# Seven batches' token norms turned block by block in the feed-forward and loaded turned in the slots' stage; the slots' keys and values put in place by masked operations

## The chip, the cores and the metric

The kernel runs as one program on one core of a Trainium2 chip. The core has five engines that run their own instruction queues: TensorE (PE, with its weight loads as PEld), VectorE (DVE), ScalarE (ACT), GpSimd (POOL) and SyncE (SP, which here only issues DMAs). SBUF is the on-chip memory of 128 partitions, PSUM holds the sums of matrix products, and 16 DMA engines move data between SBUF and DRAM. The metric is device time in microseconds (us), the median of several runs. About 0.2% is what a measurement of this kernel can tell from no change.

## The reference

Eight batches of 512 tokens of width 512 pass through a cross-attention with a feed-forward beside it, and then through a slot layer. All is float32.

```python
x = x + tanh(g_xattn) * xattn_and_ff(layernorm(x), ctx, mask, ...)   # attention over ctx, plus silu(gate) * a @ Wff2
yn = layernorm(x)                                                    # the "token norms"
# slot layer on yn: 16 slots, 16 heads of width 32
o = q + mha(slot_query, yn, yn, d_W*)          # each slot attends to all 512 tokens of its batch
h = layernorm(o) * ln_g + ln_b                 # one slot per expert
o = o + (silu(h @ W1[e] + b1) * silu(h @ Wg[e] + bg)) @ W2[e] + b2   # 16 experts of 512 x 2048
out = mha(yn, o, o, c_W*)                      # each token attends to its batch's 16 slots
x = x + tanh(g_ffn) * out
```

## The kernel before

The work is in five stages, each with its own tile pools and an order of instructions that is written out by hand (`manual_schedule`): every engine executes in exactly the order in which the program issues to it, and waits on semaphores where data are not ready.

**Cross-attention** (to about 1050 us): not touched. There is one thing in it that the prediction looks at: `spread` (L348) places 32 x 32 blocks that VectorE has transposed (L338) by small DMAs from SBUF to SBUF.

**Feed-forward** (about 1050 to 2230 us), `for s in range(NB * NFC + 2)`: 16 half batches `j` of 256 tokens, each in 16 steps of some 4.64 us, with a seven-product scheme for matrix products (L840, L864) on TensorE, and sums on VectorE. `settle(j, ...)` returns the jobs that finish half batch `j` during the steps of the next one, keyed by (step, slot): additions of the accumulators, storing of the sum (`keep_sum`), its statistics (`look`, steps 5 and 7), and `norm(t)` (steps 9 and 11, slot 1), which normalises 128 tokens in place (L129) and stores them to DRAM (`yn_kept`, L909). `due(s, slot)` issues a job between two given operations of a step. The last batch has no `norm`; it is normalised later. `settle` also has three scratch tiles `qa`, `qu`, `qw` of 128 x 256 in a pool of one buffer each.

**Slots' stage** (about 2230 to 2320 us). For each batch `b` the scores of the first half of the slots (`slot_scores`, L1179) need the norms with width on the partitions (`places[b]`, four chunks `c`), and the pooling (`slot_pool`, L1218) needs them with tokens on the partitions (`ys[b]`). `load_norm` (L1290) loads the second form from DRAM. `turn_tokens(b, t)` (L1298, L1300, L1302) makes the first out of it by four TensorE transposes for each tile of 128 tokens, and a copy from PSUM to SBUF by ScalarE or VectorE. The turns of batch `b + 1` stand between the score products of batch `b`. The probabilities are transposed by TensorE (`turn_probs`, L1208, L1209) after the third chunk of the next batch's scores. In between, `fetch()` (L1129 and L1125) loads the first pieces of the experts' weights, 2 MB each, into a ring of four buffers; one of the four (`early`) first holds two batches' norms.

**Experts** (about 2320 to 2795 us): 96 pieces of 2 MB stream through the ring (six buffers after a while); each consumed piece issues the next `fetch`. Beside it TensorE does the second half of the slots (`late_slots`, in two-advance steps per piece) and, from advance `SWITCH` to `LAST`, the tokens' queries (`token_queries`, L1487). The last fetches load the matrices of the output attention: `(cwk, cwv)`, `(cwo, bdk)` and `(bdv)`, where `bdk` and `bdv` are block-diagonal forms that start as zeros, written by GpSimd (`memset`, L1136).

**Output attention** (about 2795 us to the end): `slot_side` projects the slots to keys and values (L1672) and writes each head's 32 partitions into its place in `bdk` or `bdv`: three VectorE operations (L1686) and two ScalarE operations (L1681) per half. Then 32 tiles of 128 tokens pass through a pipeline: scores (L1719), their transposes (L1731), a softmax over the 16 slots (`token_scores` L1736 to L1738, `weights` L1744 to L1746), transposes (L1752), the output product (L1761), and `finish` (L1769, L1770).

Of the kernel before, what the change touches and what calls it, by code (L numbers as in the profile page):

```python
# [51 lines left out]
def flamingo_block(  # L52
# [678 lines left out]
    yn_kept = [keep.tile([N, D], F32, name=f"yn_kept_{b}") for b in range(B - 1)]  # L731

    with ExitStack() as sb, tc.manual_schedule(engines=ALL_ENGINES):
        NW = 4
# [143 lines left out]
        def settle(j, xr, acc):  # L878
# [27 lines left out]
            def norm(t):  # L906
                normed(xr[t], xr[t], mv[:, t, 0:1], col(rs, t))
                r = (2 * h + t) * P
                nc.sync.dma_start(yn_kept[b][r : r + P, :], xr[t])  # L909

            def step_q1():
                nc.vector.tensor_scalar(a, part(acc, 1), tg_x, None, ALU.mult)
# [33 lines left out]
            if b < B - 1:  # L946
                jobs[9, 1], jobs[11, 1] = lambda: norm(0), lambda: norm(1)
            return jobs
# [163 lines left out]
    def fetch():  # L1112
        if not pieces:
            return
        kind, e, i = piece = pieces.pop(0)
        pool, tag = buffers.pop(0)
        buffers.append((pool, tag))

        assert kind in ("w1", "wg", "w2") or pool is ring
        name = kind if kind in ("w1", "wg", "w2") else kind[0]  # L1120
        t = pool.tile([P, 8, 512], F32, tag=tag, name=f"{name}_{e}_{i}")
        if kind == "w2":

            w = e_W2[e, i * 1024 : (i + 1) * 1024, :].rearrange("(p k) d -> p (k d)", k=8)
            nc.sync.dma_start(t.rearrange("p q f -> p (q f)"), w)  # L1125
        elif kind in ("w1", "wg"):

            w = (e_W1 if kind == "w1" else e_Wg)[e, i * 256 : (i + 1) * 256, :]
            nc.sync.dma_start(  # L1129
                t.rearrange("p q f -> p (q f)"), w.rearrange("(p k) f -> p (k f)", k=2)  # L1130
            )
        else:
            for k, n in enumerate(kind):
                half = t[:, 4 * k : 4 * k + 4]
                if n in ("bdk", "bdv"):
                    nc.gpsimd.memset(half, 0.0)  # L1136
                else:
                    w = {"cwk": c_Wk, "cwv": c_Wv, "cwo": c_Wo}[n]
                    nc.sync.dma_start(half, rows(w))
                pieces_in[n, 0, 0] = half  # L1140
            return
        pieces_in[piece] = t
# [7 lines left out]
    ball = slots.tile([P, 512], F32, name="ball")  # L1150
    oT = slots.tile([P, ND, P], F32, name="oT")


# [17 lines left out]
    pooled = c1.tile([P, ND, FH, HS, B], F32, name="pooled")  # L1171
    ys, probs, pTs = {}, {}, {}

# [10 lines left out]
    def slot_scores(b, m, sp, apart=False):  # L1184

        yT = places[b].rearrange("p (c n) -> p c n", c=ND)
        for c in range(ND):
# [89 lines left out]
    with ExitStack() as sc, tc.manual_schedule(engines=ALL_ENGINES):  # L1277
        ps = sc.enter_context(tc.tile_pool(name="ps_c", bufs=2, space=PSUM, reuse_waits="tile"))

        def load_norm(b):  # L1280

            at = {4: 7, 5: B}.get(b)
            if b in (2, 3):
                y = early[:, 4 * (b - 2) : 4 * (b - 1)]
            elif at is None:
                y = c3.tile([P, NT, D], F32, tag=f"y{b % 2}", name=f"y_{b}")
            else:
                y = places[at].rearrange("p (t d) -> p t d", t=NT)
            src = yn_kept[b] if b < B - 1 else y_kept[b]
            nc.sync.dma_start(y, src.rearrange("(t p) d -> p t d", p=P))  # L1290
            return y

        def turn_tokens(b, t):
# [3 lines left out]
            for c in range(ND):  # L1297
                nc.tensor.transpose(tp[:, c, :], ys[b][:, t, c * P : (c + 1) * P], ident)  # L1298
            if (t % 2 or b == 0) and (b, t) != (1, NT - 1):
                nc.scalar.copy(yT[:, :, t * P : (t + 1) * P], tp)  # L1300
            else:
                nc.vector.tensor_copy(yT[:, :, t * P : (t + 1) * P], tp)  # L1302
# [8 lines left out]

        early = ring.tile([P, 2 * NT, D], F32, tag=buffers[RING - 1][1], name="early")
        for b in range(4):
            ys[b] = load_norm(b)
        b2r = e1.tile([NS, D], F32, tag="ys", name="b2r")
        nc.sync.dma_start(b2r, e_b2)
        nc.sync.dma_start(o, by_slot(slot_query[0]))
        nc.sync.dma_start(dbo, d_bo.partition_broadcast(P))
        ys[4] = load_norm(4)
        fetch()  # L1320
        ys[5] = load_norm(5)
        for _ in range(RING - 2):
            fetch()
        for i, bvec in enumerate((e_b1, e_bg)):
            nc.sync.dma_start(
                ball[64 * i : 64 * i + 64], bvec.rearrange("e (k f) -> (e k) f", k=4)
            )
# [7 lines left out]
        nc.scalar.activation(col(spark, 0), neg_half[:, 0:1], AF.Exp)  # L1335
        for t in range(NT):
            turn_tokens(0, t)
        for b in range(B):
# [15 lines left out]
            for t in range(NT):  # L1354
                if t == NT - 1 and b > 0:
                    turn_probs(b - 1, 0, bank4("tp", f"stp_{b - 1}"))
                next(late)
                if b + 1 < B and (b != 1 or t > 0):
                    turn_tokens(b + 1, t)
                if b == 0 and t == NT - 1:  # L1360
                    turn_tokens(2, 0)
            if b > 0:
                for _ in slot_pool(b - 1, [bank4("pl", f"pl_{b - 1}")]):
                    pass
            if b in (1, 2):
                ys[b + 5] = load_norm(b + 5)
            if b == 4:
                fetch()
# [3 lines left out]
            if b == B - 1:  # L1372
                dwo = c3.tile([P, 4, D], F32, tag="y0", name="dwo")
                nc.sync.dma_start(dwo, rows(d_Wo))
        late = slot_scores(1, 1, bank("sc", "lsc_1"), apart=True)
        for c in range(ND):
# [13 lines left out]
    with experts_scope, ExitStack() as se, tc.manual_schedule(engines=ALL_ENGINES):  # L1390
# [41 lines left out]
        def prepare():  # L1432
            for j in range(2):
                nc.vector.memset(held[j], 0.0)
            nc.vector.tensor_add(fold, ident[:, 0:32], ident[:, 32:64])
            nc.vector.tensor_add(fold, fold, ident[:, 64:96])
# [56 lines left out]

        SWITCH, LAG, LAST = 82, 6, PIECES - 1
        AHEAD = 3
# [155 lines left out]

    bdk, bdv = (t.rearrange("p g (b r s) -> p g b r s", b=B, r=4) for t in (bdk, bdv))


    with ring_scope, ExitStack() as sd, tc.manual_schedule(engines=ALL_ENGINES):
# [9 lines left out]
        def slot_side(w, bd, bias, name, half):  # L1665

            kp = ps.tile([P, 2, NS, B], F32, tag="mm", name=f"{name}_p_{half}")
            gs = slice(2 * half, 2 * half + 2)
            for i in range(2):
                g = 2 * half + i  # L1670
                for c in range(ND):
                    nc.tensor.matmul(  # L1672
                        kp[:, i].rearrange("p s b -> p (s b)"), lhsT=w[:, c, g * P : (g + 1) * P],
                        rhs=oT[:, c, :], start=(c == 0), stop=(c == ND - 1),
                    )
            for r in range(4):
                s = slice(FD * r, FD * r + FD)
                if r == 3:
                    for i in range(2):
                        g = 2 * half + i  # L1680
                        nc.scalar.activation(  # L1681
                            bd[s, g, :, r, :].rearrange("p b s -> p s b"), kp[s, i],
                            AF.Identity, bias=bias[s, g : g + 1],
                        )
                else:
                    nc.vector.tensor_tensor(  # L1686
                        bd[s, gs, :, r, :].rearrange("p g b s -> p g s b"), kp[s],
                        wide(bias[s, gs], NS, B), ALU.add,
                    )

        def slot_values(b, m):
# [4 lines left out]
            for i in range(2):  # L1696
                g = 2 * m + i
                nc.tensor.matmul(
                    vp[64 * i : 64 * i + 64, :],
                    lhsT=bdv[:, g, b].rearrange("p r s -> p (r s)"), rhs=cwo[:, g, :],  # L1700
                    start=True, stop=True,
# [3 lines left out]
        def load(i):  # L1705
            b, t = divmod(i, NT)
            xr = d7.tile([P, D], F32, tag="xr", name=f"xr_d_{i}")
            nc.sync.dma_start(xr, y_kept[b][t * P : (t + 1) * P, :])
            return xr

        def batch_scores(b, m):
# [5 lines left out]
            for i in range(2):  # L1717
                g = 2 * m + i
                nc.tensor.matmul(  # L1719
                    sp[64 * i : 64 * i + 64, :],  # L1720
                    lhsT=bdk[:, g, b].rearrange("p r s -> p (r s)"), rhs=qT[:, g, :],
                    start=True, stop=True,
# [3 lines left out]
        def token_scores(i):  # L1726
            b, t = divmod(i, NT)
            sp = ps.tile([P, FH, NS], F32, tag="sc", name=f"sc_{i}")
            spf = sp.rearrange("p h s -> p (h s)")
            for m in range(2):  # L1730
                nc.tensor.transpose(  # L1731
                    spf[:, m * P : (m + 1) * P], sTs[b][:, m, t * P : (t + 1) * P], ident
                )
            mx = d4.tile([P, FH], F32, tag="mx", name="mx")
            pr = d4.tile([P, FH, NS], F32, tag="pr", name=f"pr_{i}")
            nc.vector.tensor_reduce(mx, sp, AX.X, ALU.max)  # L1736
            nc.vector.tensor_tensor(pr, sp, wide(mx, NS), ALU.subtract)
            nc.scalar.activation(pr, pr, AF.Exp, scale=FSCALE)  # L1738
            return pr

        def weights(pr):
            den = d4.tile([P, FH], F32, tag="den", name="den_d")
            rden = d4.tile([P, FH], F32, tag="rden", name="rden_d")
            nc.vector.tensor_reduce(den, pr, AX.X, ALU.add)  # L1744
            nc.vector.reciprocal(rden, den)
            nc.gpsimd.tensor_tensor(pr, pr, wide(rden, NS), ALU.mult)  # L1746

        def turn_weights(i, pr):
            prf = pr.rearrange("p h s -> p (h s)")
            tp = ps.tile([P, 2, P], F32, tag="tp", name=f"ptp_{i}")  # L1750
# [103 lines left out]
```

## Time and profile before

| | |
|---|---|
| Time, median of 3 runs | 2927.24 us (2927.17 to 2928.19) |
| Profiled execution, its own time | 2923.94 us |
| Its span, first to last instruction | 2922.1 us |
| Granted TensorE clock, mean | 0.998 |
| Busy: PE, DVE, ACT, POOL | 2843.3, 1781.0, 833.1, 1043.3 us |
| Moved by DMA | 481.26 MB, mean 165 GB/s |

A profile's part with 40 slices shows the share of each engine's busy time by stage; TensorE is busy throughout, while the DMA engines are busy in the cross-attention, nearly idle in the feed-forward, and full from about 2330 to 2795 us. A line of the "timeline" gives start, duration, engine, line of the code, operation, output <- inputs, shapes, a count of merged instructions, and in brackets how long the engine had been idle and who released it. SPq lines are issues of DMAs, not their transfers. The merged durations of TensorE overlap, so steps are best read from start to start. A float32 product shows as two records.

### The profile page before, as it was taken

How to read it: one execution, taken by the hardware profiler on the slowest of the kernel's cores; microseconds unless marked ns; L12 is line 12 of the kernel's file. 1: busy time of each engine (PE TensorE's matmuls, PEld its weight loads, DVE VectorE, ACT ScalarE, POOL GpSimd, SP SyncE). 2: the span in 40 equal slices, each digit the busy share in tenths (PEclk: the TensorE clock that was granted, in tenths of full speed). 3: DMA queues.
4: the chain of work that ended last, by engine and by line, in shares of the span. 5: the costliest groups of instructions: out<-in, count | busy, mean ns of one | idle time of the engine just before them, and what ended most of it. 6: DMA issues, size and time to landing. Idle time of an engine off the chain costs nothing.

```text
span 2922.1 us, 49771 instructions
## 1 busy us (share of the span) xinstructions
PE 2843.3 (97%) x17822; PEld 1824.2 (62%) x17822; DVE 1781.0 (61%) x5337; ACT 833.1 (29%) x2256; POOL 1043.3 (36%) x835
## 2 busy tenths in 40 slices
PE   9999999999999999999999999999999998899898
PEld 5333333333333489999999999999998644322233
DVE  7887878878786766666666666666665312111145
ACT  4444444444444521111111111111112222000023
POOL 6888888788887671000000000000001100000034
PEclk9999999999999999999999999999999999999999
DMA  7887877778788650000000000000005399999954
GB/s 207 202 205 177 213 184 194 197 187 213 180 204 197 160 213 24 26 30 30 30 30 30 30 30 27 29 30 30 30 23 213 125 426 426 425 427 426 427 182 150
DMA packets 262584, 481.26 MB, mean 165 GB/s; under 512 B 24832, under 2 KB 195360, under 8 KB 249024
## 3 DMA queue, kind: packets, MB, share of 16 engines
q1 hardware_dynamic: 261616, 476.10, 51.5%
q8 instruction: 141, 2.31, 0.3%
q0 software_dynamic: 480, 1.57, 0.1%
q14 instruction: 107, 0.88, 0.1%
q10 hardware_dynamic: 240, 0.40, 0.1%
HBM read 303.91 MB, written 40.89 MB: 118 GB/s over the span
## 4 chain that ended last, share of the span: by engine, by line
PE 85%; DMA 11%; DVE 2%; issue 1%; SPq 1%; ACT 0%; POOL 0%; POOLq 0%; DVEq 0%; ACTq 0%
PE p L840 27%; PE acc L864 13%; DMA w<-in_L_ffn_e_W_dram 9%; PE sim L296 8%; PE qp L279 8%; PE av L374 7%; PE op L388 7%; PE out L1761 2%; PE p_w L1565 1%; PE pl L1218 1%; DMA cwk<-in_L_ffn_c_Wv_dram 1%; PE ssc L1179 1%; PE lsc L1179 1%; PE kp L250 1%; PE tp L216 1%; PE p_wg L1565 1%
## 5 line engine op out<-in xcount | busy, mean ns | idle before, releaser
L323 POOL TENSOR_SCALAR pr<-pr,rden 128x512 f32<-128x512 f32 x504 | 788.3, 1582 | 175.5 <-DVE rden L316 173.9
L310 ACT ACTIVATE pr<-pr,nmx 128x512 f32<-128x512 f32 x512 | 363.5, 711 | 375.7 <-DVE nmx L307 330.7
L307 DVE CUSTOM_DVE_ANT_0 pr<-sim,bias 128x512 f32<-128x512 f32 x512 | 322.8, 685 | 74.2 <-PE sim L296 74.2
L338 DVE STREAM_TRANSPOSE turned<-pr 128x512 f32<-128x512 f32 x504 | 322.3, 682 | 9.2 <-DMA pT<-turned 1.2
L840 PE MATMUL p<-xs,w1g 128*128 128x128 f32 x2048 | 312.3, 275 | 0.5 <-DMA w1g<-in_L_xattn_Wff_dram 0.5
L840 PE MATMUL p<-ts,s 128*128 128x128 f32 x2048 | 311.5, 275 | 0.0
L864 PE MATMUL acc<-w,ht 128*128 128x256 f32 x1024 | 305.5, 381 | 0.0
L840 PEld LDWEIGHTS p<-ts,s 128*128 128x128 f32 x2048 | 289.1, 192 | 13.0
L840 PEld LDWEIGHTS p<-xs,w1g 128*128 128x128 f32 x2048 | 279.6, 192 | 7.1 <-issue 0.6
L296 PE MATMUL sim<-kT,q 64*128 64x512 f32 x1024 | 263.8, 616 | 2.8 <-DVE nmx L307 2.5
L892 POOL TENSOR_TENSOR xr_b<-xr_b,qa 128x256 f32<-128x256 f32 x16 | 11.7, 731 | 678.7 <-DVE xr_b L889 678.7
L279 PE MATMUL qp<-xnT,wq 128*128 128x512 f32 x496 | 245.1, 618 | 0.6 <-DVE xnT L238 0.6
L374 PE MATMUL av<-pT,v 128*64 128x512 f32 x1008 | 233.3, 605 | 0.3 <-issue 0.3
L388 PE MATMUL op<-wo,o 128*128 128x512 f32 x512 | 230.6, 593 | 0.0
L864 PE MATMUL acc<-t,ht 128*128 128x256 f32 x768 | 229.1, 380 | 0.0
L296 PEld LDWEIGHTS sim<-kT,q 64*128 64x128 f32 x1024 | 91.3, 186 | 168.6 <-issue 102.2
L1072 DVE TENSOR_TENSOR c<-p,w 128x128 f32<-128x128 f32 x256 | 74.4, 291 | 179.5 <-PE p L840 179.1
L1066 ACT ACTIVATE g<-p 128x128 f32<-128x128 f32 x256 | 70.9, 277 | 388.3 <-PE p L840 388.3
L1078 ACT ACTIVATE g<-g 128x128 f32<-128x128 f32 x256 | 79.4, 310 | 354.9 <-DVE g L1077 354.9
L279 PEld LDWEIGHTS qp<-xnT,wq 128*128 128x128 f32 x496 | 84.3, 189 | 151.7 <-issue 142.6
L388 PEld LDWEIGHTS op<-wo,o 128*128 128x128 f32 x512 | 95.2, 190 | 112.6 <-issue 112.3
L840 PEld LDWEIGHTS p<-ts,w1a 128*128 128x128 f32 x1024 | 154.4, 191 | 13.3
(306 smaller groups left out, 4174.8 us busy)
## 6 DMA issues: line engine op xcount, KB each, us to landing
w<-in_L_ffn_e_W_dram SPq DMA_DIRECT2D x64, 2048.0 KB, 17.5
pT<-turned SPq DMA_DIRECT2D x1008, 128.0 KB, 2.8
wg<-in_L_ffn_e_Wg_dram SPq DMA_DIRECT2D x32, 2048.0 KB, 28.0
wq<-in_L_xattn_Wq_dram SPq DMA_DIRECT2D x64, 256.0 KB, 4.6
xn<-in_x_dram SPq DMA_DIRECT2D x32, 256.0 KB, 3.0
cn<-in_ctx_dram SPq DMA_DIRECT2D x32, 256.0 KB, 3.8
xnT_kept<-xnT SPq DMA_DIRECT2D x8, 1024.0 KB
xr<-in_x_dram SPq DMA_DIRECT2D x32, 256.0 KB, 4.8
```

The source lines that it names most:

```text
L279: nc.tensor.matmul(qp, lhsT=w[:, c, :], rhs=xnT[:, c, :], start=(c == 0), stop=(c == ND - 1))
L296: nc.tensor.matmul(sps[l, e], lhsT=qs[half * HP + l][r, t * P : (t + 1) * P], rhs=kT[r, :], start=True, stop=True,)
L307: nc.vector.tensor_tensor_reduce(pr, sps[l, e], bias, -XSCALE, LARGE, ALU.add, ALU.min, nmx)
L310: nc.scalar.activation(pr, pr, AF.Exp, bias=nmx, scale=-1.0, accum_out=dens[l][:, e : e + 1])
L323: nc.gpsimd.tensor_scalar(prs[l, e], prs[l, e], rden[:, e : e + 1], None, ALU.mult)
L338: nc.vector.transpose(turned[:, :, hd, :], pr.rearrange("p (j c) -> p j c", c=32))
L374: nc.tensor.matmul(av[XD * e : XD * e + XD], lhsT=v[:, j, :], rhs=p5[:, j, :, :, e, :], start=(j == 0), stop=(j == NT - 1),)
L388: nc.tensor.matmul(op, lhsT=o[:, l, :], rhs=wo[:, half * HP + l, :], start=(l == 0), stop=(l == HP - 1),)
L840: nc.tensor.matmul(psum[:, 0:HN], lhsT=w[:, c, :], rhs=x[:, c, :], start=(first and c == 0), stop=(last and c == 1), skip_group_check=True,)
L864: nc.tensor.matmul(part(acc, q), lhsT=ht[:, idx, :], rhs=rhs, start=(kp == 0 and half == 0), stop=(kp == NFC // 2 - 1), skip_group_check=True,
L1072: nc.vector.tensor_tensor(c22, p7[:, 0:HN], w, ALU.add)
L1078: nc.scalar.activation(g2, g2, AF.Silu)
```

## The change

1. In the feed-forward, `norm` moves one step earlier (8 and 10). A new job `turn` (steps 9 and 11) has VectorE transpose the 32 x 32 blocks of the tile's two halves into `z` tiles, which reuse the buffers of `qa` and `qu`, and stores each by four DMAs to DRAM (`yT_kept`, width by tokens). This is done for batches 0 to 6: 28 tiles, 56 transposes, 224 stores.
2. In the slots' stage, batches 0 to 6 are loaded turned (`load_turned`); only batch 7 is still turned by TensorE (16 transposes instead of 128). The loads of all tokens' norms are issued ahead of the first fetches. Batches 0 and 1 are first loaded into other buffers (`home`) and loaded once more to their places later. Two ring buffers hold the early norms instead of one; two fetches follow them, and the third and fourth come after the pooling at `b == 2` and `b == 4`.
3. `bdk` and `bdv` are no longer zeroed. `own_head`, 1 where a partition belongs to head `r` of its group and 0 elsewhere, masks the result: two VectorE operations of 128 x 512 per half write (sum + bias) x mask over whole tiles. The order within them is batch, slot, head instead of batch, head, slot, so the right side of the projections is read with a stride, and the softmax in `token_scores` and `weights` runs over a stride of four.
4. `LAST` becomes `PIECES - 3`, so the tokens' queries are spread over two advances less.

```diff
+    yT_kept = [keep.tile([D, N], F32, name=f"yT_kept_{b}") for b in range(B - 1)]
...
+            def turn(t):
+                r = (2 * h + t) * P
+                yT = yT_kept[b].rearrange("(k i) n -> i k n", i=32)
+                for i, n in enumerate("au"):
+                    z = b0.tile([P, HD], F32, tag=f"q{n}", name=f"z{n}_{j}_{t}")
+                    nc.vector.transpose(z, xr[t][:, i * HD : (i + 1) * HD])
+                    for k in range(4):
+                        nc.sync.dma_start(
+                            yT[:, 8 * i : 8 * i + 8, r + 32 * k : r + 32 * k + 32],
+                            z[32 * k : 32 * k + 32].rearrange("p (k c) -> p k c", c=32),
+                        )
...
-                jobs[9, 1], jobs[11, 1] = lambda: norm(0), lambda: norm(1)
+                jobs[8, 1], jobs[10, 1] = lambda: norm(0), lambda: norm(1)
+                jobs[9, 1], jobs[11, 1] = lambda: turn(0), lambda: turn(1)
...
-                if n in ("bdk", "bdv"):
-                    nc.gpsimd.memset(half, 0.0)
-                else:
+                if n not in ("bdk", "bdv"):
...
-        yT = places[b].rearrange("p (c n) -> p c n", c=ND)
+        yT = turned.get(b, places[b]).rearrange("p (c n) -> p c n", c=ND)
...
+        for b in (0, 1):
+            turned[b] = home(b, b)
+            load_turned(b, turned[b])
+        early = [
+            ring.tile([P, 2, NT * D], F32, tag=buffers[RING - 2 + i][1], name=f"early_{i}")
+            for i in range(2)
+        ]
         for b in range(4):
-            ys[b] = load_norm(b)
+            load_norm(b, early[b // 2][:, b % 2])
...
-        ys[4] = load_norm(4)
-        fetch()
-        ys[5] = load_norm(5)
+        load_turned(2, places[2])
+        load_turned(3, places[3])
+        load_norm(4, places[7])
+        load_turned(4, places[4])
+        load_norm(5, places[B])
+        load_norm(6, home(0, 6))
+        load_turned(5, places[5])
+        load_norm(7, home(1, 7))
+        load_turned(6, places[6])
         for _ in range(RING - 2):
             fetch()
+        for b in (0, 1):
+            load_turned(b, places[b])
...
-        for t in range(NT):
-            turn_tokens(0, t)
...
-                if b + 1 < B and (b != 1 or t > 0):
+                if b + 1 == B - 1:
                     turn_tokens(b + 1, t)
-                if b == 0 and t == NT - 1:
-                    turn_tokens(2, 0)
...
-            if b in (1, 2):
-                ys[b + 5] = load_norm(b + 5)
-            if b == 4:
+            if b in (2, 4):
                 fetch()
...
-        SWITCH, LAG, LAST = 82, 6, PIECES - 1
+        SWITCH, LAG, LAST = 82, 6, PIECES - 3
...
-            for r in range(4):
-                s = slice(FD * r, FD * r + FD)
-                if r == 3:
-                    for i in range(2):
-                        g = 2 * half + i
-                        nc.scalar.activation(
-                            bd[s, g, :, r, :].rearrange("p b s -> p s b"), kp[s, i],
-                            AF.Identity, bias=bias[s, g : g + 1],
-                        )
-                else:
-                    nc.vector.tensor_tensor(
-                        bd[s, gs, :, r, :].rearrange("p g b s -> p g s b"), kp[s],
-                        wide(bias[s, gs], NS, B), ALU.add,
-                    )
+            for i in range(2):
+                g = 2 * half + i
+                nc.vector.scalar_tensor_tensor(
+                    bd[:, g].rearrange("p b s r -> p (b s) r"),
+                    kp[:, i].unsqueeze(2).to_broadcast([P, NS * B, 4]), bias[:, g : g + 1],
+                    own_head.unsqueeze(1).to_broadcast([P, NS * B, 4]), ALU.add, ALU.mult,
+                )
...
-            nc.vector.tensor_reduce(mx, sp, AX.X, ALU.max)
-            nc.vector.tensor_tensor(pr, sp, wide(mx, NS), ALU.subtract)
+            nc.vector.tensor_reduce(mx, sp.rearrange("p g s r -> p g r s"), AX.X, ALU.max)
+            nc.vector.tensor_tensor(pr, sp, over_slots(mx), ALU.subtract)
...
-            nc.gpsimd.tensor_tensor(pr, pr, wide(rden, NS), ALU.mult)
+            nc.gpsimd.tensor_tensor(pr, pr, over_slots(rden), ALU.mult)
```

## The prediction

> **What bounds the kernel now.** I read the stages in the 40 slices first, then the table of busy time by stretches, the SP queue and TensorE in time order around the stages' borders. The two stages that the change touches behave unlike each other.
>
> ```profile
> 2240.00:2300.00 60.00, 59.69 (x373) 44.44 (x374) 23.02 (x47) 15.53 (x32) 11.98 (x8) 1.00 0.61 222
> 2300.00:2360.00 60.00, 55.06 (x578) 28.30 (x578) 16.02 (x44) 12.85 (x24) 5.26 (x4) 1.00 0.59 245
> ...
> 2600.00:2660.00 60.00, 54.01 (x516) 16.48 (x508) 8.68 (x14) 2.39 (x4) 0.00 (x0) 1.00 1.01 426
> ```
>
> The columns are the stretch, busy PE, PEld, DVE, ACT and POOL, granted clock, DMA share and GB/s. In the slots' stage (first row) TensorE is busy 59.69 of 60 us and the DMA engines 61%. In the experts (last row) the DMA engines are full at 426 GB/s. So the slots' stage is as long as its TensorE work, and the experts' as long as their bytes. What joins them is the time at which the stream of weights starts:
>
> ```profile
> 2303.71 0.37 SPq L1374 DMA_DIRECT2D dwo<-in_L_ffn_d_Wo_dram  x1
> 2327.32 0.34 SPq L1129 DMA_DIRECT2D w<-in_L_ffn_e_W_dram  x1
> 2329.04 0.34 SPq L1129 DMA_DIRECT2D wg<-in_L_ffn_e_Wg_dram  x1
> ```
>
> SP has nothing to issue from 2304 to 2327.32 us: all four ring buffers are loaded and wait for TensorE to reach the first expert. From 2327.32 the DMA share stays at 1.0 until about 2795. The bytes behind that point do not change (four pieces are ahead of it in both programs), so each us by which TensorE reaches the experts earlier shifts the whole stream and the output stage behind it by one us.
>
> **Feed-forward: 0 us.** TensorE is busy all the time; the added work lies on VectorE and SP.
>
> ```profile
> 2047.16 0.29 DVE L1068 TENSOR_TENSOR w<-p,v 128x128 f32<-128x128 f32 x1 [0.52 <-PE p L840]
> 2047.37 0.54 DVE L129 TENSOR_SCALAR xr_b<-xr_b,mvy,rsy 128x512 f32<-128x512 f32 x1
> 2048.49 0.29 DVE L1072 TENSOR_TENSOR c<-p,w 128x128 f32<-128x128 f32 x1 [0.58 <-PE p L840]
> ```
>
> This is slot 1 of step 9. Between 2047.37 and 2048.49 VectorE has 1.12 us, of which the norm takes 0.54. Now two block transposes of 128x256 stand there. The same operation at 128x512 takes 0.682 us (L338), and other 128x256 operations 0.41 (L1013), so two cost 0.7 to 0.8 and fit. In step 8 the norm (0.54) falls into 0.84 idle us ahead of the same operation (2044.07). If no cover held, 28 times 0.82 would be 23 us; I take 0, since both places are in the trace.
>
> The new wait: the second turn of a half batch rewrites the two z tiles, so VectorE waits there for the first turn's eight stores. The turns lie 9.28 us apart (norm rows at 2047.37 and 2056.65). The nearest row is the stores that place the attention's turned blocks:
>
> ```profile
> pT<-turned SPq DMA_DIRECT2D x1008, 128.0 KB, 2.8
> ```
>
> SP needs 0.60 us for each of those. Eight are issued by 0.8 + 8 x 0.6 = 5.6 us after the turn begins, and with 2.8 us to landing the last is there at 8.4; the last z is wanted at 9.28 + 0.41 = 9.7. The margin is 1.3 us. The row has runs of 1 KB and 128 KB a store, SBUF to SBUF; the new stores have runs of 128 B and 32 KB, into DRAM, and no row shows that form. Rows of stores to DRAM land in 2.0 us (y_kept, 256 KB), and the same pT row has a longest landing of 8.1 us: these are the ends. I take 2.8. Behind VectorE's wait stand the additions that TensorE waits for. On SP the eight stores come ahead of the next yn store and of the next half batch's loads (step 12, used 5 steps later), which have over 20 us.
>
> [...] What a late landing costs is the third rival.
>
> **Slots' stage: -13.6 us.** One batch's step is seen between two starts of the same product:
>
> ```profile
> 2249.12 1.02 PE L1179 MATMUL ssc<-place,qt 128*128 128x512 f32 x2
> 2249.99 0.60 PE L1298 MATMUL ytp<-ident,early 128*128 128x128 f32 x4
> 2250.42 1.02 PE L1179 MATMUL ssc<-place,qt 128*128 128x512 f32 x2
> ...
> 2254.75 3.74 PE L1218 MATMUL pl<-spT,y 128*128 128x128 f32 x32
> 2258.42 0.41 PE L1344 MATMUL b_tp<-ident,b2r 16*128 16x16 f32 x4
> ```
>
> A chunk of scores costs 0.865 us, a tile's turn 0.435 (2249.99 to 2250.42), the turn of the probabilities 0.435, the pooling 3.6. So a batch is 4 x 0.865 + 4 x 0.435 + 0.435 + 3.57 = 9.2 us, and without its turns 7.46. Batch by batch, on the profile's clock:
> - Batch 0 can start where the first turn stood, 2229.5: its turned norms are loaded at 2207.5 (the same buffer and release as y_0 now), long landed. It ends at 2232.9.
> - Batch 1: three chunks end at 2235.5. Then the probabilities of batch 0 must be ready. VectorE is in the feed-forward's last statistics until 2234.23 (L903); from its first softmax operation to the end of POOL's scaling the trace has 3.73 us (2237.63 to 2241.36), so 2238.0. TensorE stands 2.5 us, a new wait in place of 1.8 us (2238.46 to 2240.26) and of 0.9 us of first turns waiting for copies. Then 0.435 + 0.865 + 3.57: batch 1 ends at 2242.9, now at 2249.1.
> - Batches 2 to 5: 4 x 7.46 + 0.34 (b2's transposes) = 30.2, so 2273.1; now 2286.7. From one batch's scores to the turn of its probabilities lie 6.2 us, and the softmax needs 4.0 (2245.27 to 2249.26), so no further wait.
> - Batch 6 keeps batch 7's turns: 9.2, 2282.3. The rest is the same 24.2 us as now (2295.93 to 2320.10): 2306.5 instead of 2320.1.
>
> The loads: 9 MB more. Five of the new order's transfers go out from 2217.6 and fill the DMA engines at 390 to 416 GB/s (rates of 2240 to 2260) until about 2231; the turned batches 2 and 3 are issued at 2229 and land by 2237, batch 4 by 2243; needed at 2242.9, 2250.4 and 2258. The whole of tokens and pieces is 25 MB x 1.05 / 0.4 = 66 us from 2217, 2283, ahead of 2306.5. Ends of this term: -12.2 (only 28 x 0.435) to -15.
>
> **Output stage: -3.6 us.**
>
> ```profile
> 2796.77 3.62 DVE L1686 TENSOR_TENSOR cwo<-k_p,vec 32x256 f32<-32x256 f32 x6 [2.20 <-DMA cwo<-in_L_ffn_c_Wo_dram]
> ...
> 2809.72 1.08 PE L1698 MATMUL vtp<-cwo,bdv 128*64 128x512 f32 x4 [1.42 <-ACT bdv L1681]
> ...
> 2810.73 0.44 PE L1752 MATMUL ptp<-ident,pr 128*128 128x128 f32 x2
> ```
>
> Twelve VectorE operations of 0.59 us with eight of ScalarE (0.45) behind them become eight of 128x512; the same kind with PSUM input takes 0.74 (L1769), a strided 128x512 product 1.09 (L1583). I take 0.75. LAST takes the query products out of the last piece, whose eviction (0.75, 2792.48) holds up the last sum: k_p starts 1.1 earlier, 2793.5. Keys: halves end at 2795.4 and 2797.2, masked by 2796.9 and 2798.7 (scores can start at 2797.2 and 2798.8, now 2799.53 and 2801.27). Values: from 2799.7 (2802.28), masked by 2803.1 and, behind the first tile's maximum, 2805.4; second vtp at 2805.5 instead of 2809.72, and ptp at 2806.8 instead of 2810.73. So 4.0 us. The 32 tiles then go at 3.31 us each (PE L1761 from start to start), TensorE's time; VectorE does 2.24 of it and POOL 1.9. A strided copy takes 1.09 against 0.69 (L1225, L1302); if the strided reductions grew alike, VectorE would reach 2.7, still covered, but the last tiles' chain is bare: +0.4 or so. The removed memsets (2 x 1.80, POOL) end long before they are wanted: 0. The 32-byte stride of oT on the right side appears in no row. The experts' weights are read there in 16-byte pieces as fast as whole rows (L1565 and L1179, 1.72 us for 16 records each), so I take 0; the upper end is a doubling, second rival.
>
> **Sum.** 0 - 13.6 - 4.0 + 0.4 = -17.2 us. The profiled execution took 2923.94 (span 2922.1), 3.3 below the median, so the sum would be 2906.7 there, and 2927.24 - 17.2 = **2910** for the median.
>
> **Rivals.**
> - *Forecast*, 2910 (2905 to 2916), 72%.
> - *Strided reads cost* (12%): the key and value products (3.85 + 3.9 us, 2794.63 on and 2802.28 on) double on the path. The output stage turns from -3.6 to +4: 2918. For it: unknown form; against it: the 16-byte row.
> - *Stores land late* (8%), the slower end: if the last landing takes 8.1 us instead of 2.8, it is there at 13.7, VectorE waits 4.0, some 0.5 of which the gaps hide, 14 times (once per half batch): +49, 2959. The gain is eaten when a stop costs 17.2 / 14 = 1.2 us, from a landing of 5.8 us. Against: the feed-forward moves 30 GB/s, while 8.1 is from a stage at 190. [...]
> - *The slots' stage becomes bound by loads* (8%): if the 9 MB more delay the third and fourth pieces or a turned batch so far that the 13.6 is lost, only the output stage is left: 2924. For it: a DMA share of 0.61 there already; against it: the margins of 7 to 25 us above.
>
> That the change does not do what it says is ruled out by the built program: 112 transposes fewer, 224 stores, 9 turned loads.
>
> The range is 2904 to 2925: it takes in the first, second and fourth and leaves out the third. 0.2% is 5.9 us, about what can be told from no change: faster 0.85 (72 + 10 + 3), same 0.07 (2 + 5), slower 0.08.
>
> **What would show it.** The start of the stream (2327.32) at about 2313.7; score products back to back, one 2.5 us stop in batch 1; VectorE at the second turn without a wait on a yT store; the masking rows at 0.75; k_p and v_p still 3.9 us a pair; 3.31 us a tile. A feed-forward longer than 74.2 us per half batch would make the forecast wrong, and so would a stop at the turned loads.

## The result and the profile after

The changed kernel takes 2918.93 us (median of 9 runs, 2917.21 to 2922.94) where the kernel before takes 2927.24 (2924.84 to 2928.19 over 9 runs): ratio 0.9977, 95% interval 0.9968 to 0.9986, or 8.3 us faster. 17.2 had been forecast. The profiled execution took 2920.0 (span 2918.2), 1.1 above its median; that of before was 3.3 below its own. In both profiles I set each stage against the start of that stage, because untouched stages differ from run to run: the feed-forward ends 3.05 us later in the profile after (2232.52 against 2229.47), and the same 3.04 us already lie between two loads of xs long ahead of it (1115.20 against 1112.16), where the change touches nothing.

The feed-forward. Its half-batch from 1189.40 to 1263.60 in the profile after, in the table of busy time by stretches (stretch, busy PE, PEld, DVE, ACT, POOL, granted clock, DMA share, GB/s), and then the turning line by itself (count, shortest, median and longest in ns):

```profile
1189.40:1263.60 74.20, 74.20 (x561) 71.31 (x560) 47.59 (x175) 13.65 (x48) 3.76 (x5) 1.00 0.13 36
```

```profile
L919 DVE STREAM_TRANSPOSE za<-xr_b x28: 435/435/435, 1160.0 to 2133.9; 128x256 f32<-128x256 f32 x28
L919 DVE STREAM_TRANSPOSE zu<-xr_b x28: 403/403/403, 1160.4 to 2134.2; 128x256 f32<-128x256 f32 x28
its engine sat idle before it (us, times) until:
who waited for it (us, times):
```

TensorE is busy for all of the 74.20 us, which is the period of before. The 56 turns take 0.42 us each, and the list of what VectorE waited for ahead of them is empty: the eight stores have always left the two tiles. The eight are issued in 3.8 to 4.9 us, and a store lands 1.7 us after its issue in the median, 3.7 at the longest.

The slots' stage. TensorE in order of time, profile after:

```profile
2241.15 0.66 PE L1225 MATMUL stp<-ident,spr 128*128 128x128 f32 x4 [2.46 <-POOL spr L1217]
2241.64 1.02 PE L1196 MATMUL ssc<-y,qt 128*128 128x512 f32 x2
2242.52 3.84 PE L1235 MATMUL pl<-spT,early 128*128 128x128 f32 x32
...
2310.43 1.07 PE L1574 MATMUL p_w<-ball,ident 128*32 128x256 f32 x16
2313.01 1.07 PE L1574 MATMUL p_wg<-ball,ident 128*32 128x256 f32 x16 [1.50 <-ACT o L1290]
```

The last two lines are the first expert's bias products. In the profile before they stand back to back:

```profile
2320.10 1.07 PE L1546 MATMUL p_w<-ball,ident 128*32 128x256 f32 x16
2320.98 1.05 PE L1546 MATMUL p_wg<-ball,ident 128*32 128x256 f32 x16
```

The one stop of 2.46 us in batch 1 is there, and from then on batches follow one another without a stop. At the bottom of the view after is a stop that the kernel before does not have: the second bias product waits 1.50 us for ScalarE's copy of the slots' output (2312.37 to 2312.95). The first weight fetch follows at 2319.37, 86.85 us after the feed-forward's end, where before it was 97.85: 11.0 us gained.

The output stage, same view, first before and then after:

```profile
2789.63 1.92 PE L1609 MATMUL yq<-w,held 128*32 128x512 f32 x16 [0.75 <-DMA w<-in_L_ffn_e_W_dram]
...
2794.63 3.84 PE L1672 MATMUL k_p<-oT,cwk 128*128 128x128 f32 x32 [0.38 <-DVE oT L1534]
2802.28 2.05 PE L1672 MATMUL v_p<-oT,cwk 128*128 128x128 f32 x16
2804.38 1.95 PE L1672 MATMUL v_p<-oT,cwk 128*128 128x128 f32 x16
```

```profile
2782.05 3.42 PE L1637 MATMUL yq<-w,held 128*32 128x512 f32 x16 [2.08 <-DMA w<-in_L_ffn_e_W_dram]
2785.94 1.09 PE L1558 MATMUL y_tp<-fold,ys 128*128 128x32 f32 x8 [0.47 <-ACT ys L1554]
2787.41 7.70 PE L1699 MATMUL k_p<-oT,cwk 128*128 128x128 f32 x32 [0.38 <-DVE oT L1562]
...
2797.82 3.97 PE L1699 MATMUL v_p<-oT,cwk 128*128 128x128 f32 x16
...
2801.85 3.89 PE L1699 MATMUL v_p<-oT,cwk 128*128 128x128 f32 x16
```

The key products take 7.70 us instead of 3.84 and the value products 3.97 + 3.89 instead of 2.05 + 1.95. The last product with the experts' weights (first line of each) takes 3.42 instead of 1.92. The clock speaks to both; the stretches of the same profile:

```profile
2782.00:2784.00 2.00, 1.95 (x12) 0.59 (x16) 0.00 (x0) 0.00 (x0) 0.00 (x0) 0.58 1.03 378
...
2790.00:2792.00 2.00, 2.00 (x10) 2.00 (x10) 0.58 (x1) 0.00 (x0) 0.00 (x0) 0.50 0.81 259
...
2802.00:2806.00 4.00, 4.00 (x21) 3.38 (x21) 2.22 (x5) 0.42 (x1) 0.00 (x0) 1.00 0.00 0
```

The granted clock is 0.58 and 0.50 in stretches from 2782 to 2792, and 1.00 while the values are multiplied. So two causes were possible for the long k_p, and only one for the long v_p.

Stage by stage, profile against profile (k_p to the first ptp is the part with the masking):

| stretch | before | after | change | forecast |
|---|---|---|---|---|
| half batch of the feed-forward | 74.20 | 74.20 | 0 | 0 |
| end of feed-forward to first fetch | 97.85 | 86.85 | -11.0 | -13.6 |
| first fetch to last weight product | 462.31 | 462.68 | +0.4 | 0 |
| last weight product to k_p | 5.00 | 5.36 | +0.4 | -1.1 |
| k_p to first ptp | 16.10 | 21.41 | +5.3 | -2.9 |
| first ptp to the end | 111.4 | 109.4 | -2.0 | +0.4 |

The last row is not the change's: in the profile of before the last tiles' additions on POOL wait for late loads of tokens (a stop of 2.2 us in all), and the kernel of the second experiment, which has that stage as before, shows 109.4 too. It is not constant either: the profiles of the experiments have 108.9 to 113.2 there. Without that row the table adds up to -4.9; the medians say -8.3, with an interval of 4.1 to 9.4. In two later series of runs the kernel before had medians of 2925.97 and 2925.88, by which the change would be worth 7.0. The 2.1 to 3.4 us between the table and these numbers I cannot assign to a line. The interval reaches down to 4.1, so noise is not ruled out; but the turned tokens alone, below, have a surplus of the same size (12.9 by the medians, 10.6 by the stages).

### The profile page after: what moved, and what is told of

Its sections match the earlier page's. It is cut to its first block, busy times and chain, and to the rows that moved or that the text cites. A ratio compares the mean times of both kernels' runs of the same rounds, so it can differ in the third digit from the quotient of the medians.

```text
span 2918.2 us, 49933 instructions
## 1 busy us (share of the span) xinstructions
PE 2843.3 (97%) x17710; PEld 1820.9 (62%) x17710; DVE 1793.6 (61%) x5381; ACT 822.7 (28%) x2233; POOL 1042.7 (36%) x833
```

## The experiments

My theory after the traces: the order (b s) of the right side, 32 bytes from element to element, doubles the key and value products, 7.6 us on the path. The rival: the fallen clock made k_p long. Beside these, the two smaller losses: the bank at the experts' start and the queries taken out of the last pieces.

### Straight right side

```
-  oT[:, c, r_].rearrange("p (s b) -> p s b", b=B),
+  oT[:, c].rearrange("p (b s) -> p s b", b=B)[:, m * HS : (m + 1) * HS],
...
-  own = oT[:, :, g0 : g0 + 32]
-  nc.vector.tensor_add(own, own, yp)
+  own = oT.rearrange("p c (b s) -> p c s b", b=B)[:, :, g0 // B : g0 // B + 4]
+  nc.vector.tensor_add(own, own, yp.rearrange("p c (s b) -> p c s b", b=B))
...
-  rhs=oT[:, c, :].rearrange("p (s b) -> p b s", b=B), ...
+  rhs=oT[:, c, :], ...
```

> The changed kernel with one thing undone: the columns of oT are written slot-minor where they are made, so that the key and value products read their right side in whole rows again (the masking rows and everything else stay). Stride theory: k_p falls from 7.70 to 3.85 us and v_p from 3.97 + 3.89 to 2.0 + 2.0, all of it on the path: 2918.9 - 7.7 = about 2911. Rival, the clock: the granted clock was 0.50 to 0.58 in places from 2782 to 2792 us, and k_p is long because of it; then k_p changes only as the clock does, v_p (at 1.00) does not change at all, and the time stays at about 2919.

2911.97 us (2907.26 to 2914.94); against before 0.9954 (0.9942 to 0.9967). TensorE in order of time:

```profile
2780.48 3.59 PE L1637 MATMUL yq<-w,held 128*32 128x512 f32 x16 [2.08 <-DMA w<-in_L_ffn_e_W_dram]
...
2786.09 3.84 PE L1699 MATMUL k_p<-oT,cwk 128*128 128x128 f32 x32 [0.46 <-DVE oT L1562]
2792.63 2.05 PE L1699 MATMUL v_p<-oT,cwk 128*128 128x128 f32 x16
2794.74 1.95 PE L1699 MATMUL v_p<-oT,cwk 128*128 128x128 f32 x16
```

Both pairs are back at the times of before, and k_p to the first ptp is 13.77: 7.64 less than with the strided side, and 2.33 less than before, which is what the masking itself gives. The rival is out for the 7.6: v_p was doubled at a clock of 1.00. The slow last weight product is still there; it has another cause.

### Each part alone

The turned tokens alone, with the output stage and LAST as before; against the changed kernel, the core of the diff:

```
-        SWITCH, LAG, LAST = 82, 6, PIECES - 3
+        SWITCH, LAG, LAST = 82, 6, PIECES - 1
...
-                        rhs=oT[:, c, :].rearrange("p (s b) -> p b s", b=B), ...
+                        rhs=oT[:, c, :], ...
...
-                nc.vector.scalar_tensor_tensor(
+                    nc.vector.tensor_tensor(
```

> Only the first part of the change: the norms turned in the feed-forward and loaded in the slots' stage; keys, values, softmax layout and the order of the query products as before. Theory: the first weight fetch comes 11 us earlier after the end of the feed-forward and nothing behind it changes: 2927.2 - 11 = about 2916. Rival (stores land late, or loads bound the stage): part of the 11 us is given back in the feed-forward (a half batch longer than 74.20 us) or in the stream; 2920 or more.

2913.07 us (2912.34 to 2913.36); against before 0.9957 (0.9945 to 0.9970). A half batch of the feed-forward takes 74.20 us as before. From the feed-forward's end to the first fetch it is 86.84 us, from there to the last weight product 462.72, to k_p 5.00, k_p 3.84: the 11.0 us of the profile, and nothing given back. This half of the change alone is faster than the whole.

The masking alone, with the strided right side, the tokens turned by TensorE; against the kernel before, the core of the diff:

```
-                        rhs=oT[:, c, :], ...
+                        rhs=oT[:, c, :].rearrange("p (s b) -> p b s", b=B), ...
...
-                    nc.vector.tensor_tensor(
+                nc.vector.scalar_tensor_tensor(
```

> Only the second part: masked keys and values, the slot-major layout of the softmax, with the strided right side; tokens turned by TensorE as before, query products up to the last piece as before. Stride theory: products 7.75 us longer, evictions 3 to 4 us shorter: about 4 us slower than before, 2931. Forecast of the prediction: 2.5 to 3.6 us faster, 2924.

2929.75 us (2927.0 to 2933.07); against before 1.0013 (1.0005 to 1.0022). The interval lies above 1, but by less than the 0.2% that I trust a comparison of times with; the trace decides. k_p 7.70, v_p 3.97 + 3.89, k_p to the first ptp 21.40 against 16.10: the +5.3 of the table.

This run bears on the rival too. Its queries go up to the last piece and TensorE stands only 0.75 us for the last weights, as before; still the clock falls in the middle of k_p, to a mean of 0.71 from 2795 to 2798 and 0.81 from 2798 to 2802.4, with TensorE busy in all of both stretches, where the kernel before has 1.00. So with a strided right side the clock falls in k_p without a longer stand ahead of it than before.

### The banks of the slots' stage

In the kernel before, the transposes ask for their two PSUM banks first; with the first turns gone, the scores do, and the last scores' bank holds the slots' output when the experts start. One line asks for a transposes' bank ahead of the loop:

```
+        bank4("tp", "tp_first")
         for b in range(B):
```

> The changed kernel with the PSUM banks of the slots' stage given out in the old order (the transposes' banks first, then the scores'). Theory: the first expert's bias product then waits for a bank that was free long before, instead of for ScalarE's copy of the slots' output; its stop of 1.50 us goes, the first fetch comes 1.7 us earlier: about 2917.3. Rival: the stop only moves, because the next product (of the normed slots) waits for the same chain; then the fetch comes at the same place and the time stays at 2919.

2917.14 us (2913.69 to 2922.66); against before 0.9972 (0.9962 to 0.9981), which the times cannot tell from the changed kernel. In the trace the two bias products stand back to back (2306.48 and 2307.37), and from the first of them to the fetch it is 7.22 us, as before the change, instead of 8.94. The 1.7 us is confirmed. On its other side the first scores wait 0.88 us for VectorE to leave their bank, and the stop in batch 1 is shorter by more (1.32 instead of 2.46). Counted from the end of the feed-forward's products, with the 0.88 us, the fetch comes after 84.98 us instead of 86.85.

### How far apart may the elements be

```
+  step = {("k", 0): 2, ("k", 1): 4, ("v", 0): 16}.get((name, half))
...
+  right = (
+      oT[:, c, :].rearrange("p (s b) -> p b s", b=step) if step
+      else oT[:, c, :].rearrange("p (s b r) -> p b s r", b=4, r=2)
+  )
```

> The changed kernel, with the columns of the right side read in another order in each of the four groups of products (so which slot and batch a key or value belongs to is not the reference's): first half of the keys one element in 2 (8 bytes apart), second half one in 4 (16 bytes), first half of the values one in 16 (64 bytes), second half pairs of elements 32 bytes apart. A half takes 1.95 us where rows are whole, 3.9 at 32 bytes. [...] Rival: any broken row costs the double, 3.9 in all four. Second rival: the cost grows with the distance, about 2.4, 2.9, 5 or more, and 2.9 for the pairs.

```profile
2785.90 2.09 PE L1704 MATMUL ka_p<-oT,cwk 128*128 128x128 f32 x16 [0.38 <-DVE oT L1562]
2787.82 3.81 PE L1704 MATMUL kb_p<-oT,cwk 128*128 128x128 f32 x16
...
2794.34 3.73 PE L1704 MATMUL va_p<-oT,cwk 128*128 128x128 f32 x16
2798.13 2.01 PE L1704 MATMUL vb_p<-oT,cwk 128*128 128x128 f32 x16
```

One run: 2915.08 us. From the top: elements 8, 16 and 64 bytes apart, then pairs 32 bytes apart; the granted clock is 1.00 in the stretches from 2786 to 2798, over the first three rows. At 8 bytes the row takes 2.09 us, as whole rows do (2.05 and 1.95 for v_p in the kernel before); at 16 bytes 3.81, at 64 bytes 3.73, beside 3.97 and 3.89 at 32 bytes in the changed kernel; the pairs take 2.01. So it is neither "any broken row" nor the distance: both rivals are out. What the rows go with is how many elements are taken from each 16 bytes that are read from: two cost nothing, one costs double. The 16 is a way of counting that fits these rows. No run has a step between 8 and 16 bytes, and none shows why a single element costs more.

### The queries in the last pieces

```
-        SWITCH, LAG, LAST = 82, 6, PIECES - 3
+        SWITCH, LAG, LAST = 82, 6, PIECES - 1
```

> The changed kernel with the token queries spread up to the last piece again, as before. Clock theory: without queries in the last two pieces TensorE stood 2.08 us for the last weights and the clock fell to 0.58, so the last product took 3.42 instead of 1.92 us; with the queries back it stands under 1 us, the product takes 1.92, and k_p starts 5.0 us after it instead of 5.4: time 2918.5, 0.4 less. Forecast of the prediction for this step: taking the queries out saved 1.1 us, so this kernel would be 1.1 slower, 2920. The times cannot tell 0.4 from 1.1; the distance from the last product to k_p and the clock there can.

2920.16 us (2917.3 to 2923.97), against before 0.9978 (0.9969 to 0.9986): not to be told from the changed kernel. The trace tells it:

```profile
2778.94 1.93 PE L1637 MATMUL yq<-w,held 128*32 128x512 f32 x16 [0.69 <-DMA w<-in_L_ffn_e_W_dram]
...
2783.94 7.71 PE L1699 MATMUL k_p<-oT,cwk 128*128 128x128 f32 x32 [0.38 <-DVE oT L1562]
```

With queries to the last piece TensorE stands 0.69 us for the weights instead of 2.08, the product takes 1.93, and k_p comes 5.00 us after it instead of 5.36. So the step that I put at -1.1 costs 0.4 here. The saving itself is there: from the end of the last product to k_p it is 1.94 us in the changed kernel and 3.07 here, 1.13 less. The product that grew by 1.50 us has eaten it.

k_p takes 7.71 as in the changed kernel. Its clock has another course here (1.00 until 2786, 0.57 from there to 2790), but the mean over k_p is 0.78 in both, so this equality alone shows nothing. The value products do: 3.97 + 3.89 us for as many records at a clock of 1.00. And in the changed kernel the records of k_p take 411 ns at the shortest and 412 in the median, within one k_p that has both 1.00 and 0.50; those of v_p, at 1.00, also take 412 in the median. In these runs the read with one element from each 16 bytes takes as long at 0.50 as at 1.00.

### Together, and the clock once more

The diffs of the straight right side and of the banks together:

> Slot-minor oT and the banks of the slots' stage in the old order together, in the changed kernel. If both gains are separate places on the path they add: 2918.9 - 7.0 - 1.8 = about 2910. If the earlier stream only waits elsewhere: 2912.

The same with `LAST = PIECES - 1`:

> As the one before, with the token queries spread up to the last piece as before the change. Clock theory: no fall of the clock at the last piece, k_p 0.4 us nearer to the last product: 2909.6 against 2910. The prediction's forecast for this step: 1.1 us slower, 2911.

2909.13 us (2905.51 to 2916.03), ratio 0.9937 (0.9925 to 0.9949), and 2908.33 us (2905.89 to 2912.88), ratio 0.9938 (0.9926 to 0.9950): both beat both kernels, and they can't be told from each other by time. In their traces they can. First the one with the queries ended early, then the other:

```profile
2783.78 3.62 PE L1638 MATMUL yq<-w,held 128*32 128x512 f32 x16 [2.04 <-DMA w<-in_L_ffn_e_W_dram]
...
2789.44 5.47 PE L1700 MATMUL k_p<-oT,cwk 128*128 128x128 f32 x32 [0.46 <-DVE oT L1563]
```

```profile
2778.29 1.92 PE L1638 MATMUL yq<-w,held 128*32 128x512 f32 x16 [0.72 <-DMA w<-in_L_ffn_e_W_dram]
...
2783.38 3.84 PE L1700 MATMUL k_p<-oT,cwk 128*128 128x128 f32 x32 [0.47 <-DVE oT L1563]
```

From the last weight product to the end of k_p it is 11.13 us in the first (5.66 + 5.47) and 8.93 in the second (5.09 + 3.84). In the first the clock is 0.50 at 2784 to 2786 and 0.69 in the mean of k_p; in the second it is 1.00 throughout. With whole rows a low clock does reach k_p. It need not: the straight right side alone, above, also ends its queries early and has a slow last product, but its clock was back at 1.00 for k_p, and the distance is 9.45 us. So what LAST costs differs from kernel to kernel.

The same with `LAST = PIECES - 2`:

> Slot-minor oT and the old order of banks, with the token queries spread up to the last piece but one: half the step between the two kernels before. If the clock falls only after a stand of about 2 us, the stand ahead of the last product is 1.2 to 1.6 us here, the product takes 1.92 and k_p 3.84, and k_p starts about 4.6 us after the product, 0.4 less than with queries to the last piece. If any longer stand is enough, the product takes over 3 us again.

One run: 2910.97 us (the kernel before beside it: 2930.59). The stand was 1.04 us and the product took 1.92, and k_p started 3.97 us after it, which is the saving of 1.0 with a product that is not slowed. But k_p took 5.46, at a clock of 0.50 and 0.68 from 2782 to 2786: neither of my two expectations. The distance to the end of k_p is 9.43 us, between the two others. So a stand of 2 us right ahead is not what is needed; the clock also fell, at about 2782, behind a stretch in which TensorE was busy 2.6 us of 4 (2776 to 2780).

In steps of 0.2 us the trace of the changed kernel shows more. Each of its two falls is a step down to 0.50 that lasts 3.4 us (2782.3 to 2785.7 and 2789.2 to 2792.6), and the second begins 6.8 us after the first, twice that length. The means over stretches of 2 and 3 us in the other traces give the same, if each fall is one step to 0.50: 3.4 us here (2781.9 to 2785.3), and 2783.8 to 2787.2 and 2790.6 to 2794.0 in the version with the queries ended early, again 6.8 us apart. What starts a fall, the traces do not show. The longest of these stands for the last weights is 2.09 us. How little work makes the clock fall stays open: 2.9 us busy of 4 around the start of k_p (2780 to 2784, with queries to the last piece) keeps 1.00.

### The stop in batch 1

Batch 1's fourth score product put ahead of the turn that waits, in the version with all gains:

```
-                if t == NT - 1 and b > 0:
+                if t == NT - 1 and b > 1:
                     turn_probs(b - 1, 0, bank4("tp", f"stp_{b - 1}"))
                 next(late)
...
+            if b == 1:
+                turn_probs(0, 0, bank4("tp", "stp_0"))
             if b > 0:
```

> Slot-minor oT, the old order of banks, queries to the last piece, and batch 1's fourth score product put ahead of the turn of batch 0's probabilities, into the stop in which TensorE waits for them. The stop is the softmax chain's and not TensorE's: it falls by the product's 0.865 us, from 1.31 to about 0.45, and the first fetch comes 0.87 us earlier after the start of the stage (84.10 to 83.2). If the bank of the scores or another wait held it, nothing moves.

One run: 2912.9 us (before, the same 2930.59).

```profile
2228.17 7.13 PE L1196 MATMUL ssc<-y,qt 128*128 128x512 f32 x16 [0.88 <-DVE xr_b L891]
2235.77 0.66 PE L1225 MATMUL stp<-ident,spr 128*128 128x128 f32 x4 [0.46 <-POOL spr L1217]
2239.46 5.47 PE L1235 MATMUL pl<-spT,early 128*128 128x128 f32 x32 [3.04 <-ACT spT L1226]
```

The stop fell to 0.46 as expected, and a new one of 3.04 us stands behind it. ScalarE's copy of the turned probabilities (2238.85) now comes behind the exponentials of batch 1 (2238.12), because the program now issues it behind them, and the trace has the two in that order; and the exponentials come late, because VectorE starts on the scores only at 2236.98, by the profile behind POOL's addition to o. TensorE's pooling then runs at a mean clock of 0.69 and takes 5.47 instead of 3.84. The fetch comes 88.06 us after the stage's start instead of 84.10. The expectation failed: the product that looked like work to be moved into the gap had covered the copy behind it (2239.55 to 2240.14 in the version with all gains), and the move changed ScalarE's order too. Which of the two costs more, no run separates. One run each tells nothing of the time; the trace carries this.

## Why the prediction was right and wrong

Right: the feed-forward costs nothing. The stop in batch 1 was forecast at 2.5 and is 2.46. The masking rows take 0.70 to 0.75 us (0.75 forecast), and the 32 tiles keep their 3.31 us although the strided sums grew from 0.41 to 0.65 us (`den_d`): the cover held. No store came late: landing was 1.7 us, with 2.8 taken and 5.8 as the point of danger. The loads did not bound the stage, and the stream is 462.7 us long against 462.3.

Wrong, in order of size:

- **"The experts' weights are read there in 16-byte pieces as fast as whole rows, so I take 0."** This is the step that failed, 7.64 us. The row was right and did not bear on the case: a piece of 16 bytes gives four elements from each 16 bytes, the new right side one. In the rows of the fifth experiment two are enough (2.09 and 2.01 us) and one is not (3.81 and 3.73), so the nearest row lay on the other side of the edge. The rival *strided reads cost* (12%) had mechanism and price: 7.75 us forecast, 7.64 measured.
- **Slots' stage, -13.6:** -11.0 measured. 1.7 us of the gap is the bank stop, a wait that no line of the diff names: the order in which the tiles are first asked for decides which bank the next stage inherits. The other 0.9 lies within the stage, mostly in batches of 7.58 us (2261.91 to 2269.49) where I had 7.46.
- **LAST, -1.1 within the output stage's -4.0:** +0.4 measured. The eviction that goes is worth the 1.1 that I counted (1.94 us behind the last product instead of 3.07). I did not count the work that goes: without queries TensorE stands 2.08 us before the last weights, its clock falls to 0.50, and the last product takes 1.50 us more.
- **Masking, -2.9 without LAST:** -2.33, a small miss of size. **Reductions, +0.4:** not seen.

With the terms as measured (-11.0, +0.4 of the stream, +0.4, -2.33 + 7.64) the sum is the -4.9 of the table; the 2.1 to 3.4 us beyond it in the medians stay unassigned. The version without the three losses is at 2908 us, where the forecast for this change had been 2910. That is partly luck: by the stages of its trace it gains 14.5 us of the 17.2, and the unassigned surplus fills the rest. The rival's total of 2918 lies beside the measured 2918.93 by luck too: it still held the slots' stage at -13.6.

## What to carry to other kernels

Before a matmul's operand is read in another order, count how many elements it takes from each 16 bytes (16 records took 2.01 to 2.09 us here with two, 3.73 to 3.97 with one), and put the permutation where few elements are written (here a dozen small additions) instead of where many are read. When tiles go from a stage, look at which bank or buffer the next stage gets: the order of first requests is part of the change (1.7 us here). Small work beside a wait is not free to be removed or moved: where the queries went, the clock fell to 0.50 and the last product took 3.42 and 3.62 us instead of 1.93 and 1.92, and where the score product was moved, ScalarE's copy behind it came late and a stop of 3.04 us stood there.

## What the runs showed of the hardware

- A float32 right side costs 0.94 ns a column and record in whole rows (3.84 us for 32 records of 128 columns, two records to a product), the same with two elements from each 16 bytes (2.01 to 2.09 us for 16 records, 1.95 to 2.05 in whole rows), and 1.88 with one, at 16, 32 and 64 bytes alike (3.73 to 3.97 us for 16 records). A low clock lengthens the first (5.47 us at a mean of 0.69) and not the second (7.70 us at a mean of 0.78, 3.97 + 3.89 at 1.00).
- Where the clock fell in the changed kernel, it was 0.50 for 3.4 us each time, and the two falls began 6.8 us apart; with the straight right side and the old order of banks the means of the stretches give the same. It also fell within strided products during which TensorE's records leave no gap (a mean of 0.71 from 2795 to 2798 and 0.81 from 2798 to 2802.4 with the masking alone).
- VectorE's sum over 128x256 with a step of 16 bytes takes 0.65 us from SBUF instead of 0.41; the maximum with the same step from PSUM stays at 0.42.
- Stores of 32 KB into DRAM in runs of 128 bytes land in 1.7 us, sooner than those of 256 KB with long runs (2.0), at 36 GB/s on the DMA engines. For each byte they take about 2.2 times the engines' time of the other transfers: over the same 890 us of the feed-forward the queue's share is 12.7% for 31.47 MB, and before 8.2% for 25.17 MB.
